# The planner's prices of transfers in a four-layer kernel: larger fixed part, lower rates

## Chip, core and metric

The kernel runs on one core of a Trainium2 chip. The metric is the device time of one execution in microseconds (us); the median of the runs is compared. TensorE is called PE, VectorE DVE, ScalarE ACT, GpSimd POOL and SyncE SP.

## What is computed

Four layers over `x`, 2 sequences of 1024 tokens with 128 features, all in float32. Each layer has the same frame:

```python
xn = _layernorm(x)
s = attention_like(xn)             # layer 0 Mamba scan, 1 linear attention, 2 SSD (chunked state space), 3 causal attention
g = _silu(feed_forward(xn))        # layers 0, 1, 2: experts, two of eight for each token; 3: a plain two-layer net
x = x + s * g
```

What matters for transfers lies in layers 0 and 2. In layer 0 the recurrence runs over 256 channels with 16 states each:

```python
dA = jnp.exp(dt_s[..., None] * A)
h = h * dA + (dt_s * x_s)[..., None] * B_s[:, None, :]
y = jnp.einsum('bds,bs->bd', h, C_s)
```

In layer 2 there are 32 heads of 64 channels, 128 states, and chunks, with a decay matrix inside a chunk and a state handed from chunk to chunk:

```python
M = Gm * Lmat
Y_diag = jnp.einsum('bclsh,bcshp->bclhp', M, h_c)
states = jnp.einsum('bhij,bjhpn->bihpn', dc, states)[:, :-1]
Y_off = jnp.einsum('bclhn,bchpn->bclhp', C_c, states) * sdo[..., None]
```

## The kernel before

**The work.** Tokens lie in 16 tiles of 128 (`X`). Layer 0 first normalises and routes, then scans four half sequences of 512 tokens (`inputs` and `step`, sixteen steps for each). A step needs 128 rows that are 32 channels times 4 states, so its operands are written to DRAM and read back replicated: `Dtd` (step width and its product with the input, stored at L1087, read into `dd` at L1230, for the very first ones straight from SBUF at L1228) and `BCd` (B and C, stored at L1056, read into `bc` at L1235). ACT makes `dA` (L1251), DVE `dBx` (L1243; every fourth on POOL, L1241) and the scan `hs` (L1252), POOL multiplies by C (L1256), PE folds the states (L1263). The experts of layer 0 (weights `fw`, L1133) run between the steps, and from the third half sequence on layer 1 of the first sequence too (weights `w13f` L775 and `w2e` L778).

Layer 2 works through 32 blocks of two heads (16 for each sequence) in pairs: `front` (projection, convolution; weights `wf` L1664, whose split halves are stored as `parts` at L1668 and read back by the second sequence at L1672), `weights` (decay rows `Srow` L1692 and `Mrow` L1693 are read from DRAM, PE makes `e_ps`, ACT its exponential, DVE `M`), `states` (`cd` L1712 is read replicated, DVE scans `st` at L1735) and `tail` (`so` L1751 is read replicated, then `yd_ps`, `yo_ps`, and every fourth block `wo_ps`). The next pair's `front` and `weights` are written before the present pair's `tail`. `Vd`, `Cd`, `So` and `Dd` are the DRAM tensors that these reads come from (L1537 to L1552). `gb` (L1810) reads the gate at the end of a sequence.

**Who sets the order.** Every transfer is issued on SP's queue. The order written in the program is only a start: `_issue_order` replaces it. It takes all instructions (`_operations`), with their dependences and a price for each (`_price` for engines; for a transfer also `op.wire`, its time on a wire that the plan shares out to one transfer at a time). `_forward` is a list scheduler: it plays the program by these prices, takes the ready instruction with the smallest key on every engine, opens a tile's buffer when its former user is done, and keeps a shared wire. `_backward` plays it from the end and gives each instruction its time to the end, which becomes the next round's key. Thirty such rounds are followed by 300 tries in which the keys within a stretch of 60 us are shaken at random; the order with the shortest planned time is kept, for all five queues, and the chip must follow it queue by queue.

A transfer's price has a fixed part, `_DMA`, and its bytes over a rate in bytes per ns. There are four kinds: one that doesn't replicate, one that replicates out of SBUF (`dd` from `dt`), one that replicates out of DRAM with more than two distinct rows (`bc` with 4, `dd` with 32), and one that does so with one or two (`so` with 1, `cd` with 2, broadcast parameter rows). A part of `_DMA` comes ahead of the wire and the rest behind it. `_backward` uses `_DMA + op.wire`. SP's own time for an issue is 500 ns, unchanged.

Of the kernel before, what the change touches and what calls it, by code (L numbers as in the profile page):

```python
# [72 lines left out]
_SAME = {"PE": -160.0, "DVE": 50.0, "Activation": 50.0, "Pool": 100.0, "SP": 0.0}  # L73
_TABLE = 1283.0
_SWITCH = 4000.0
_DMA = 1550.0
_SPELL = 3413.0
_LOW, _HIGH = 0.45, 0.8

# [11 lines left out]
def _table_of(ins):  # L91
    if ins.opcode != "Activation" or ins.func in (AF.Identity, AF.Copy, AF.Relu, AF.Abs, AF.Square):
        return None
    return "Exp" if ins.func in (AF.Exp, AF.Tanh) else str(ins.func)


def _elements(ap):
    n = 1
    for _, c in list(ap)[1:]:
        n *= c  # L100
    return n
# [51 lines left out]
def _operations(nc, slots):  # L153

    ops, users, past = [], {}, {}

    def in_psum(a):
        return a.tensor.name in slots and slots[a.tensor.name][3] == "PSUM"

    for ins in nc.cur_bb.bb.instructions:  # L160
        if type(ins).__name__.startswith("BassTile") or ins.opcode == "RegisterMove":
            continue
        op = _Op(len(ops), ins)
        reads, writes = ([a.bass_ap for a in x if getattr(a, "bass_ap", None) is not None] for x in (ins.ins, ins.outs))
        op.cost = _price(op, reads, writes, in_psum)
        op.table = _table_of(ins)
        op.columns, op.first, op.mate = set(), op, None
        if ins.opcode == "Matmult" and not ins.is_transpose and writes[0].ap[0][1] in (8, 32, 64):
            op.strip, op.area = writes[0].offset // (writes[0].ap[0][0] or 1), 1.0
            op.columns, op.strips = {(op.strip, writes[0].offset)}, {op.strip}  # L170
        op.wire = 0.0
        if op.dma:

            n, rows = 4, 1
            for _, c in writes[0].ap:
                n *= c
            again = any(s == 0 and c > 1 for s, c in reads[0].ap)
            for s, c in list(reads[0].ap)[:-1]:
                rows *= c if s else 1
            inside = reads[0].tensor.name in slots and slots[reads[0].tensor.name][3] != "DRAM"  # L180
            op.wire = n / (430.0 if not again else 200.0 if inside else 300.0 if rows > 2 else 170.0)
        for a, writing in [(a, False) for a in reads] + [(a, True) for a in writes]:
            name = a.tensor.name
            if name not in slots:
                continue
            space = slots[name][3]
            ap = [tuple(v) for v in a.ap]
            p0, p1, f0 = 0, 0, a.offset
            if space != "DRAM":
                row = _elements([(0, 0)] + [(0, d) for d in list(a.tensor.shape)[1:]])  # L190
                p0, f0 = divmod(a.offset, row)
                p1 = p0 + ap.pop(0)[1] - 1
            f1 = f0 + sum(abs(s) * (c - 1) for s, c in ap)
            if space == "PSUM":
                p0, p1, f0, f1 = 0, 127, 0, 4095
            log = past.setdefault(name, [])
            for q0, q1, g0, g1, other, wrote in log:
                if (writing or wrote or space == "PSUM") and other is not op and q0 <= p1 and p0 <= q1 and g0 <= f1 and f0 <= g1:
                    if other.engine != op.engine or other.dma:
                        lag = 0.0 if other.dma else _HOP[op.engine]  # L200
                    else:
                        lag = _SAME[op.engine] if wrote and not writing and op.engine != "PE" else -_AHEAD[op.engine]
                    op.after[other] = max(op.after.get(other, -1e3), lag)
            if writing:
                log[:] = [r for r in log if r[4] is op or not (p0 <= r[0] and r[1] <= p1 and f0 <= r[2] and r[3] <= f1)]
            log.append((p0, p1, f0, f1, op, writing))
            if name not in op.tiles:
                op.tiles.append(name)
                users.setdefault(name, []).append(op)
                if users[name][0] is not op:  # L210
                    op.after.setdefault(users[name][0], -1e3)

        mate = ops[-1] if ops else None
        if op.columns and mate is not None and mate.columns and mate.tiles[-1] == op.tiles[-1] and not mate.columns & op.columns:
            op.columns |= mate.columns
            if op.strip in mate.strips:
                op.cost += 10.0
            else:
                op.strips |= mate.strips
                op.cost = 25.0  # L220
            first = mate.first
            first.after.update({o: max(lag, first.after.get(o, -1e3)) for o, lag in op.after.items() if o.at < first.at})
            mate.mate, op.first = op, first
        ops.append(op)
    for op in ops:
        if op.columns and op.mate is None:
            op.cost += 87.0
    return ops, users
# [30 lines left out]
def _forward(ops, users, slots, behind, key):  # L259
# [22 lines left out]
    table, wire, port = None, 0.0, {"DVE": [0.0, 0.0], "Pool": [0.0, 0.0]}  # L282
    clock, spell, worked = 1.0, 0.0, 0.0

    def met(op, when):
        early[op] = max(early[op], when)
        need[op] -= 1
        if not need[op]:
            heapq.heappush(events, (early[op], 0, op.at, op))
# [17 lines left out]
    while events:  # L307
        now, kind, _, op = heapq.heappop(events)
        if kind == 2:
            for t in op.tiles:  # L310
                left[t] -= 1
                if not left[t]:
                    k = slots[t][:2]
                    free[k] += 1
                    freed[k].append(t)
                    open_tiles(k, now)
                    in_pool[k[0]] -= 1
                    if not in_pool[k[0]]:
                        for j, i in behind:
                            if j == k[0]:  # L320
                                waits[i] -= 1
                                for q in tags:
                                    if q[0] == i:
                                        open_tiles(q, now)
            continue
        e = op.engine
        if kind == 0:
            heapq.heappush(ready.setdefault(e, []), (key[op], op.at, op))
        if not ready.get(e) or idle.get(e, 0.0) > now:
            continue  # L330
        mate = orders[e][-1].mate if orders.get(e) else None
        held = [r for r in ready[e] if r[2] is mate] if mate is not None else []
        if held:
            op = mate
            ready[e].remove(held[0])
            heapq.heapify(ready[e])
        elif e == "PE" or e not in ("Activation", "DVE"):
            op = heapq.heappop(ready[e])[2]
        else:
            op = _next(ready[e], table, [max(0.0, t - now) for t in port["Pool"]] if e == "DVE" else (0.0, 0.0))  # L340
        cost = op.cost
        if op.table not in (None, table):
            table, cost = op.table, cost + _TABLE
        if op.lock:
            cost += max(0.0, *(port["Pool" if e == "DVE" else "DVE"][k] - now for k in op.lock))
            for k in op.lock:
                port[e][k] = now + cost
        if e == "PE":
            while now >= spell + _SPELL:
                clock = (1.0 if worked > _LOW * _SPELL else 0.5) if clock == 1.0 else (1.0 if worked > _HIGH * _SPELL else 0.5)  # L350
                spell, worked = spell + _SPELL, 0.0
            cost /= clock
            worked += cost * op.area
        start[op] = now
        orders.setdefault(e, []).append(op)
        idle[e] = now + (cost if e == "PE" or op.dma else max(cost - _AHEAD[e], 40.0))
        done = now + cost + (_AHEAD[e] if e == "PE" else 0.0)
        if op.dma:
            wire = max(wire, now + 0.4 * _DMA) + op.wire
            done = wire + 0.6 * _DMA  # L360
        end[op] = done
        for t in op.tiles:
            if t not in begun:
                begun.add(t)
                open_tiles(slots[t][:2], now)
        heapq.heappush(events, (idle[e], 1, op.at, op))
        heapq.heappush(events, (done + _HOP["PE"], 2, op.at, op))
        for other, lag in follow[op]:
            met(other, max(now, done + lag))
# [1678 lines left out]
```

## Time and profile before

| | |
|---|---|
| Median of 3 runs | 1190.09 us (1188.87 to 1194.23) |
| Profiled execution | 1188.86 us, its span 1187.1 us |
| Mean granted clock of PE | 0.939 |
| Instructions in the trace | 18167, of them 416 issues of transfers |
| Moved by DMA | 109.09 MB, 92 GB/s on average |
| HBM read, written | 91.52 MB, 14.29 MB |

The stages, as the trace shows them: 0 to 98 us loads, norms and routing; 98 to 450 the scan with the experts of layer 0 and the first sequence of layer 1; 450 to 560 layer 1's second sequence; 560 to 680 the passage into layer 2; 680 to 1100 its blocks; 1100 to 1187 layer 3.

How to read the lines that follow: Lnnn is a line of the kernel, a name such as `dd<-Dtd` is what is written and what is read, and SPq is SP's queue, which issues and waits but does no work. A row of waits names the one who waited, who ended the wait, the total in us, the number of times and the longest. The chain of waits is followed back from the last instruction, at each step to what released it.

| transfer | issues | KB each |
|---|---|---|
| `bc<-BCd` | 32 | 512 |
| `cd<-Dd` | 32 | 512 |
| `so<-So` | 64 | 256 |
| `dd<-Dtd` | 28 | 512 |
| `w13f`, `fw`, `w2e` | 16 each | 256, 192, 128 |
| `parts<-w_in_h`, `parts<-w_in_l` | 16 each | 128 |
| `Srow<-Cd`, `Mrow<-Vd` | 32 each | 16, 64 |

### The profile page before, as it was taken

How to read it: one execution, taken by the hardware profiler on the slowest of the kernel's cores; microseconds unless marked ns; L12 is line 12 of the kernel's file. 1: busy time of each engine (PE TensorE's matmuls, PEld its weight loads, DVE VectorE, ACT ScalarE, POOL GpSimd, SP SyncE). 2: the span in 40 equal slices, each digit the busy share in tenths (PEclk: the TensorE clock that was granted, in tenths of full speed). 3: DMA queues.
4: the chain of work that ended last, by engine and by line, in shares of the span. 5: the costliest groups of instructions: out<-in, count | busy, mean ns of one | idle time of the engine just before them, and what ended most of it. 6: DMA issues, size and time to landing. Idle time of an engine off the chain costs nothing.

```text
span 1187.1 us, 18167 instructions
## 1 busy us (share of the span) xinstructions
PE 1020.7 (86%) x6399; PEld 735.6 (62%) x6399; DVE 931.5 (78%) x1537; ACT 866.1 (73%) x1294; POOL 739.2 (62%) x776
## 2 busy tenths in 40 slices
PE   3997967979376889989779789999998999998998
PEld 2664523435033666778658576867676777776787
DVE  6734798997899896675776488888888999888666
ACT  4556785785877894574847689888898988877654
POOL 6564598895987375232151158797995978899311
PEclk9998997999567989999959899999999999999999
DMA  3003445352552113020030333445354444442000
GB/s 109 8 21 101 125 120 182 123 186 99 189 177 83 51 62 100 1 82 23 5 106 32 87 100 96 111 119 149 101 141 95 125 107 112 107 111 73 19 9 28
DMA packets 58846, 109.09 MB, mean 92 GB/s; under 512 B 6274, under 2 KB 31746, under 8 KB 58628
## 3 DMA queue, kind: packets, MB, share of 16 engines
q1 hardware_dynamic: 58756, 107.93, 31.6%
q8 instruction: 51, 0.84, 0.3%
q14 instruction: 39, 0.32, 0.1%
HBM read 91.52 MB, written 14.29 MB: 89 GB/s over the span
## 4 chain that ended last, share of the span: by engine, by line
PE 34%; DVE 10%; ACT 9%; issue 4%; DMA 3%; POOL 2%; SPq 0%; POOLq 0%; DVEq 0%; ACTq 0%
PE wo_ps L1781 4%; PE yd_ps L1757 3%; PE u_ps L1734 3%; PE yo_ps L1762 3%; DVE h L1419 2%; PE e_ps L1698 2%; PE y_ps L799 2%; DVE st L1735 2%; PE ht_ps L1719 1%; DMA so<-So 1%; PE y_ps L1895 1%; PE y_ps L1646 1%; PE av_ps L1925 1%; ACT e_ps L1699 1%; DVE M L1701 1%
## 5 line engine op out<-in xcount | busy, mean ns | idle before, releaser
L1256 POOL TENSOR_TENSOR hs<-hs,bc 128x512 f32<-128x512 f32 x128 | 161.0, 1278 | 48.6 <-DVE hs L1252 28.8
L1419 DVE SCALAR_TENSOR_TENSOR h<-in_ps,w,h 128x1023 f32<-128x1023 f32 (+2 forms) x96 | 121.1, 1271 | 5.7 <-ACT h L1416 5.5
L1251 ACT ACTIVATE dA<-dd,negA 128x512 f32<-128x512 f32 x128 | 87.4, 688 | 31.8 <-DVE hs L1252 25.4
L1735 DVE TENSOR_TENSOR_SCAN st<-cd,u_ps 128x512 f32<-128x512 f32 x64 | 77.8, 1215 | 19.4 <-PE u_ps L1734 8.7
L1701 DVE SCALAR_TENSOR_TENSOR M<-e_ps,GT 128x1024 f32<-128x1024 f32 x64 | 77.0, 1214 | 10.5 <-ACT e_ps L1699 10.3
L1768 POOL TENSOR_TENSOR h<-h,so 128x384 f32<-128x384 f32 (+1 forms) x64 | 73.0, 1144 | 19.1 <-DVE so L1767 18.6
L1769 POOL TENSOR_TENSOR h<-h,sg 128x512 f32<-128x512 f32 x64 | 82.9, 1300 | 0.8
L1252 DVE TENSOR_TENSOR_SCAN hs<-dA,last,dBx 128x512 f32<-128x512 f32 x64 | 79.9, 1271 | 2.9 <-ACT dA L1251 2.0
L799 PEld LDWEIGHTS y_ps<-w2e,hh 128*128 128x128 f32 x512 | 72.4, 199 | 14.7 <-DVE hh L791 3.8
L799 PE MATMUL y_ps<-w2e,hh 128*128 128x128 f32 x512 | 78.1, 288 | 1.9 <-DVE acc L804 0.9
L1723 POOL TENSOR_TENSOR hdd<-htok,dtd 128x512 f32<-128x512 f32 x64 | 67.1, 1051 | 20.3 <-ACT htok L1722 15.4
L1774 POOL TENSOR_TENSOR ssq<-ssq,so 128x512 f32<-128x512 f32 x60 | 76.6, 1286 | 3.0 <-ACT so L1773 2.9
L1757 PE MATMUL yd_ps<-M,htok 128*64 128x128 f32 x1024 | 70.7, 280 | 8.0 <-DVE M L1701 5.6
L1252 DVE TENSOR_TENSOR_SCAN hs<-dA,dBx 128x512 f32<-128x512 f32 x64 | 75.7, 1211 | 2.1 <-ACT dA L1251 1.1
L1734 PEld LDWEIGHTS u_ps<-hdd,Btok 128*128 128x128 f32 x448 | 63.3, 193 | 16.8 <-issue 6.0
L1762 PE MATMUL yo_ps<-Cf,stc 128*128 128x128 f32 x448 | 70.7, 280 | 2.1 <-DVE h L1765 0.9
L1734 PE MATMUL u_ps<-hdd,Btok 128*128 128x128 f32 x448 | 69.8, 281 | 2.8 <-POOL stc L1737 1.3
L1762 PEld LDWEIGHTS yo_ps<-Cf,stc 128*128 128x128 f32 x448 | 62.3, 191 | 13.4 <-issue 4.7
L1757 PEld LDWEIGHTS yd_ps<-M,htok 128*64 128x64 f32 x1024 | 55.1, 137 | 24.4 <-issue 7.0
L1243 DVE TENSOR_TENSOR dBx<-dd,B_ps 128x1024 f32<-128x1024 f32 x48 | 57.9, 1209 | 12.2 <-PE xz_ps L623 4.7
L1699 ACT ACTIVATE e_ps<-e_ps 128x1024 f32<-128x1024 f32 x64 | 64.3, 1011 | 1.9 <-PE e_ps L1698 1.4
L1263 PE MATMUL y_ps<-hs,fold 128*32 128x512 f32 x256 | 52.9, 758 | 14.1 <-DVE ln_t L591 9.2
(535 smaller groups left out, 3190.7 us busy)
## 6 DMA issues: line engine op xcount, KB each, us to landing
bc<-BCd SPq DMA_DIRECT2D x32, 512.0 KB
cd<-Dd SPq DMA_DIRECT2D x32, 512.0 KB
so<-So SPq DMA_DIRECT2D x64, 256.0 KB
dd<-Dtd SPq DMA_DIRECT2D x28, 512.0 KB
w13f<-in_w13d_dram SPq DMA_DIRECT2D x16, 256.0 KB
Dtd<-dt SPq DMA_DIRECT2D x7, 512.0 KB
fw<-in_fwd_dram SPq DMA_DIRECT2D x16, 192.0 KB
dd<-dt SPq DMA_DIRECT2D x4, 512.0 KB
```

Of the source, the lines that this page charges most:

```text
L799: nc.tensor.matmul(y_ps[:, j * P : (j + 1) * P], hh[:, c, j * P : (j + 1) * P], w2e[:, c * P : (c + 1) * P], start=(c == 0), stop=(c == 1))
L1251: nc.scalar.activation(dA, dd[:, r, 0, :], AF.Exp, scale=negA[:, n, r : r + 1])
L1252: nc.vector.tensor_tensor_scan(hs[:, r, :], dA, dBx[:, r, :], last[:, n, r : r + 1] if h else 0.0, ALU.mult, ALU.add)
L1256: nc.gpsimd.tensor_tensor(hs[:, r, :], hs[:, r, :], cs[:, 0, :], ALU.mult)
L1419: nc.vector.scalar_tensor_tensor(dst[:, n:], ps[:, : S - n], w[:, k : k + 1], dst[:, n:], ALU.mult, ALU.add)
L1701: nc.vector.scalar_tensor_tensor(M, ps, 3.0e38, G, ALU.min, ALU.mult)
L1734: nc.tensor.matmul(pv[:, j, :], Btok[:, c, :], hdd[:, c, :], start=True, stop=True)
L1735: nc.vector.tensor_tensor_scan(st.rearrange("p f j -> p (f j)"), cd[:, half].rearrange("p h w -> p (h w)"), ps, 0.0, ALU.mult, ALU.add)
L1757: nc.tensor.matmul(yd[64 * k : 64 * (k + 1), j * P : (j + 1) * P], htok[:, 4 * q + j, 64 * k : 64 * (k + 1)], Ms[q][:, k, j * P : (j + 1) ...
L1762: nc.tensor.matmul(yo[:, j * P : (j + 1) * P], stc[:, c - 1, :], Cf[:, c * P : (c + 1) * P], start=True, stop=True)
L1769: nc.gpsimd.tensor_tensor(y, y, sg[:, cols], ALU.mult)
L1774: nc.gpsimd.tensor_tensor(ssq[:, cols], ssq[:, cols], so[:, cols], ALU.add)
```

## The change

The fixed part of a transfer's price goes from 1550 to 2150 ns. The rates go from 430 to 300 (not replicated), from 200 to 190 (replicated out of SBUF) and from 300 to 230 (replicated out of DRAM, over two rows); 170 for one or two rows stays. Of the fixed part, 0.6 instead of 0.4 now lies ahead of the wire: 1290 ns instead of 620 ahead of it and 860 instead of 930 behind it. Nothing else in the program is touched; the prices act through the order that `_issue_order` writes.

```diff
-_DMA = 1550.0
+_DMA = 2150.0
...
-            op.wire = n / (430.0 if not again else 200.0 if inside else 300.0 if rows > 2 else 170.0)
+            op.wire = n / (300.0 if not again else 190.0 if inside else 230.0 if rows > 2 else 170.0)
...
         if op.dma:
-            wire = max(wire, now + 0.4 * _DMA) + op.wire
-            done = wire + 0.6 * _DMA
+            wire = max(wire, now + 0.6 * _DMA) + op.wire
+            done = wire + 0.4 * _DMA
```

## Prediction

> **What bounds the kernel now.** The page first, for the whole span: the engines' busy time and the share of the 16 DMA engines that the program's one transfer queue takes.
>
> ```profile
> PE 1020.7 (86%) x6399; PEld 735.6 (62%) x6399; DVE 931.5 (78%) x1537; ACT 866.1 (73%) x1294; POOL 739.2 (62%) x776
> q1 hardware_dynamic: 58756, 107.93, 31.6%
> ```
>
> No engine is full and the wires are a third used, so an average says little. The second view cuts the span into stages (columns: length, busy time of PE, weight loads, DVE, ACT, POOL, granted clock, DMA share, GB/s).
>
> ```profile
> 98.00:450.00 352.00, 268.98 (x1314) 147.59 (x1313) 295.86 (x380) 269.28 (x438) 264.13 (x229) 0.85 0.39 126
> 560.00:680.00 120.00, 97.44 (x593) 78.65 (x592) 78.41 (x176) 79.17 (x119) 27.10 (x36) 0.85 0.20 58
> 680.00:1100.00 420.00, 398.01 (x2898) 304.01 (x2897) 366.31 (x418) 359.16 (x467) 341.41 (x332) 1.00 0.42 109
> ```
>
> In layer 2 (680 to 1100) PE is busy 398 of 420 us at full clock: at most 22 us can be won from waits there. In the scan of layer 0 (98 to 450) DVE leads with 296 of 352 us. In the passage into layer 2 (560 to 680) nobody is full and the clock is 0.85. The third view is the waits, those that a landing transfer ended, summed (us, times, longest):
>
> ```profile
> ACT w_in_h L609 <- DMA so<-So: 7.3, 1, 7.3
> POOL u L1007 <- DMA BCd<-bc_rows: 6.1, 1, 6.1
> ACT dA L1251 <- DMA dd<-dt: 6.0, 1, 6.0
> DVE dBx L1243 <- DMA dd<-Dtd: 4.3, 3, 2.6
> ```
>
> PE has no such row. Going through the engines' idle times of 0.7 us and over one by one, 22 were ended by a landing, 61 us over all engines. Fourth, the chain that ended last; its transfers of 3 us or more (start, length) are these six, 33 us together, which is the page's "DMA 3%":
>
> ```profile
> 462.71 4.30 DMA w<-in_w_dram
> ...
> 661.05 3.18 DMA so<-So
> ...
> 723.38 4.75 DMA so<-So
> ...
> 827.72 4.92 DMA cd<-Dd
> ...
> 902.34 8.88 DMA gb<-g2d
> ...
> 1037.54 7.07 DMA so<-So
> ```
>
> The chain begins only at 436 us (its shares add to 62%). Around these links PE was mostly busy with other work: 9.8 of 10 us at 457 to 467, 9.5 of 10 at 1036 to 1046, 6.4 of 8 at 826 to 834. They are links of waiting, not 33 us to be won.
>
> **The change, part by part.** No instruction is added or removed; every one keeps its operands. Only the prices by which the planner orders the five queues change, so all that can move is order: who stands before whom on PE, DVE, ACT, POOL and SP.
>
> Prices. A transfer of n bytes cost 1550 ns plus n over its rate; now 2150 ns plus n over a lower one. Times in us from issue, old to new: `bc` and `dd` from DRAM (512 KB, 300 to 230) 3.30 to 4.43; weights `w13f` (256 KB, 430 to 300) 2.16 to 3.02; `gb` (512 KB) 2.77 to 3.90; `dd` from SBUF (200 to 190) 4.17 to 4.91; `parts` (128 KB) 1.85 to 2.59; `Srow` (16 KB) 1.59 to 2.20. `cd` and `so`, 96 transfers and the longest in layer 2, keep 170, since their source has one or two rows: 4.63 to 5.23 and 3.09 to 3.69. Not all kinds slow down.
>
> What the trace says of these prices: I took from its semaphore records, per transfer, the time from the start of the issue to the last landing. Medians: `bc` 4.06 (3.88 where nothing else was in flight), `dd` from DRAM 5.29, `so` 6.32 (shortest 3.43), `cd` 5.87 (shortest 4.65), `w13f` 2.94, `dd` from SBUF 9.0, `gb` 3.74 and 8.9, `parts` of the high halves 1.93, `Srow` 1.59. With the planner's formula put on the recorded issue times, its one shared wire included, the old prices end before the real landing in 89% of the transfers (median 0.7 us too early), the new ones in 35% (median 0.3 us too late). The old ones fit stores and tiny loads on an idle wire; the new ones fit loads under company. So consumers that the old plan puts too early will mostly stand later, and loads are asked for earlier.
>
> The Trainium skill speaks against the rates: "DMA: Bandwidth & Descriptors", section "Anatomy of one DMA — SWDGE (gpsimd) path", fits 2.0 us plus bytes over 436 GB/s (for GpSimd's path), an estimate of 3.2 us for `bc`. By it the fixed part should rise and the rates stay, and the sum below would keep only its fixed parts; the 3.88 us measured here for `bc` is above it.
>
> Against the new prices there is the wire: over the scan the old rates price its transfers at about 135 us (`bc` 56, `dd` 59, `Dtd` 8.5, weights some 11), and the DMA share of 0.39 times 352 is 137. The new rates make it about 176. Over the whole span it is 411 old, 484 new and 375 recorded (31.6% of 1187.1). The new plan spaces loads wider than the wire needs; the cost of that is in the rivals.
>
> The sum. An idle time that a landing ended shrinks at most by what its transfer's price rose, and counts where nothing covers it. In the scan: ACT's `dA` 5.96 at 118.1 (rise 0.74), DVE's `dBx` 1.52 and 2.60 and POOL's 1.57 and 2.95 at 158 to 197 (rise 1.13 each): 0.74 + 4 x 1.13 = 5.3 us. I count it in full, since DVE, ACT and POOL feed one another step by step there. In layer 2 and its entry: `w_in_h` 7.32 behind `so` (0.60), `so` 0.85 behind `cd` (0.60), `gb` 2.67 (1.13), `h` 1.77 behind `w_in_h` (0.74), `so` 0.70 and 1.47 (0.60 each): 4.3 us. PE runs through most of them, so I count half, 2.1. The other eleven idle times (first loads, `BCd` 6.06 at 98.0, weights of later layers) have rises that add to about 10 us; I count none: the loads stand at the front of SP's queue already or PE has work. Sum: -7.4 us, bounds 0 (all of it covered) and -19 (all 22 count). What is late next there is DVE in the scan and PE in layer 2, so no more than this follows.
>
> At nothing I cost: the overpriced `parts`, `Srow` and `Mrow`. They are hidden by the look-ahead, in which block pair k+2's weights are made under pair k's tails; without that cover it would be 0.6 us for each of 16 pairs, 9.6 us. Also at nothing, the moves of SP's issues themselves (0.3 to 0.5 us each): SP stands idle for most of the span.
>
> The profiled execution took 1188.86, 1.76 over its span of 1187.1, and lies 1.2 below the median of 1190.09. 1188.86 - 7.4 = 1181.5, on the median's footing 1182.7: 1183, the case's own range 1171 (-19) to 1192 (+2).
>
> **Rivals.** The slower one: a queue blocked at its head. SP issues in order, and its own waits are long already:
>
> ```profile
> SPq L1133 <- PE p L1154: 111.6, 11, 42.0
> ...
> SPq L1235 <- POOL hs L1256: 101.3, 25, 10.5
> ```
>
> A dearer load is asked for earlier; where its buffer is still read, it stands at the head of SP's queue, and every transfer behind it waits, first `BCd`, `Dtd`, `dd` and `bc` at the three changes of half sequence in the scan. The planner knows when a buffer comes free only by its own prices; the rival decides when a buffer is freed later than planned by more than the roughly 1 us by which the load was moved up. Its price is read from the two waits already seen at such a place, 6.06 (`BCd`) and 5.96 (`dd` from SBUF): two of three boundaries give 12 us, 1202. One alone gives 1196. All three give 18 us, and if PE falls to half clock meanwhile for three of the 3.41 us windows in which the trace shows its clock to change (at most 1.7 us of its work lost in each), 1213. For it: POOL and DVE in the scan have no slack to catch up. Against it: most of these waits, 42 us among them, delay nobody now.
>
> The second: the waits only change their name. Where PE or DVE leads, a transfer that lands in time lets the next instruction wait for PE or DVE. The -7.4 shrinks to within 2 us: 1190 (1188 to 1192). For it speaks PE's 95% in layer 2; against it the scan, where DVE sits idle 56 us. That the plan stays as it was is not possible in full, since every transfer's price enters every key; that it changes little in layer 2, because `so` and `cd` keep their rate, belongs to this case.
>
> **How the numbers follow.** About 0.5%, 6 us, is what a measurement of this kernel can tell from no change: faster means below 1184, slower above 1196. Forecast 0.58 (below 1184 0.36, near 0.20, slower 0.02, its centre lying close to the line); the waits renamed 0.10, all near; the blocked queue 0.32, all slower. That makes 0.36, 0.30 and 0.34. The forecast's range of 1171 to 1192 holds about half of all chance; up to 1210 it takes in most of the blocked queue, and no more than 2 in 10 is left out.
>
> **What would show it.** Right: idle time ended by landings falls from 61 to about 45 us, `dA`'s wait for `dd` and `dBx`'s waits shrink by about 1 us each, the scan ends some 5 us earlier, PE's time in layer 2 stays at 398 us. Blocked queue: SP rows for L1133, L1230 or L1235 with single waits of over 10 us just ahead of a scan step, and ACT or DVE idle behind `dd` or `bc` for more than 6 us. Renamed: the landing waits fall and the stages keep their lengths. Wrong altogether: the landing waits stay and a stage without transfers moves by more than 6 us, the last one (1100 to 1187, DMA share 0.06) above all; then order among compute instructions, which these rows can't price, made the time.

## The result, and the profile after

The changed kernel takes 1201.59 us (median; 1190.32 to 1209.67), the kernel before 1188.47 (1182.81 to 1198.96) in the same comparison: a ratio of 1.0092, 95% interval 1.0066 to 1.0118. The ratio leaves out the three slowest executions of the changed kernel; the two medians alone would give 1.011. Slower by 0.9%: outside the forecast's own 1171 to 1192 us, within the 1210 us that the prediction allowed for its rivals, and on the side that had 0.34. The profiled execution of the changed kernel took 1195.42 us, its span 1193.7: 6.6 us over the span before, and itself 6 us below its kernel's median.

The page of the changed kernel, busy times, the transfer queue and the chain by engine:

```profile
PE 1022.3 (86%) x6399; PEld 739.0 (62%) x6399; DVE 937.7 (79%) x1537; ACT 869.8 (73%) x1296; POOL 738.5 (62%) x776
q1 hardware_dynamic: 58756, 107.93, 30.6%
PE 42%; ACT 17%; DVE 15%; issue 6%; POOL 3%; DMA 1%; SPq 0%; POOLq 0%; DVEq 0%; ACTq 0%
```

The work is the same to within 6.2 us for each engine; the packets took no longer (30.6% against 31.6%). Transfers fell from 3% of the chain to 1%. The waits that a landing ended (us, times, longest), answering to those shown before:

```profile
ACT dA L1251 <- DMA dd<-dt: 9.8, 2, 5.5
ACT w_in_h L609 <- DMA so<-So: 7.1, 1, 7.1
ACT fw_h L609 <- DMA fw<-in_fwd_dram: 5.7, 4, 3.0
DVE dBx L1243 <- DMA dd<-dt: 5.0, 1, 5.0
```

`BCd` (6.1) and `dd<-Dtd` (4.3) are gone from the list; what is left stands at the scan's entrance, behind `dd` from SBUF, which took 9.0 us in the trace before and which the new price of 4.91 us still undershoots. There the waits grew: `dA`'s from 6.0 to 9.8 us, and `dBx` has one of 5.0 that was not in the list before. Over all engines the idle times of 0.7 us and over that a landing ended went from 61.0 us (22 of them) to 47.9 (15). Now the stages, cut where each trace has them: scan (first to last `hs`), layer 2 (first `e_ps` to last `wo_ps`), layer 3. First the kernel before, then the changed one (length, busy time of PE, weight loads, DVE, ACT, POOL, granted clock, DMA share, GB/s):

```profile
126.70:447.80 321.10, 246.94 (x1229) 133.76 (x1232) 285.55 (x361) 252.78 (x413) 250.87 (x204) 0.85 0.37 124
...
671.90:1100.80 428.90, 404.82 (x2929) 308.65 (x2930) 371.29 (x422) 367.20 (x475) 344.26 (x335) 0.99 0.42 107
1100.80:1187.10 86.30, 78.26 (x549) 69.07 (x547) 57.61 (x167) 48.13 (x77) 14.91 (x24) 0.99 0.07 19
```

```profile
125.10:443.90 318.80, 247.05 (x1247) 137.19 (x1247) 285.93 (x370) 254.99 (x415) 251.83 (x204) 0.87 0.37 127
...
670.60:1103.00 432.40, 404.09 (x2924) 307.14 (x2924) 373.46 (x422) 372.53 (x479) 343.93 (x333) 1.00 0.40 106
1103.00:1193.70 90.70, 81.50 (x553) 71.05 (x552) 57.34 (x167) 48.88 (x77) 15.83 (x26) 0.98 0.06 18
```

Up to the first `e_ps` the changed kernel is 1.3 us ahead (670.6 against 671.9). Then it loses 3.5 us in layer 2 and 4.4 in layer 3. In layer 2 PE is busy as long and stands idle longer (432.4 - 404.1 = 28.3 us against 24.1). In layer 3 most of the loss is busy time: nearly the same number of matmuls took 81.5 us instead of 78.3, at a granted clock of 0.98 instead of 0.99, and the idle time went from 8.0 to 9.2 us. Layers 2 and 3 together: 515.2 us before, 523.1 after. Layer 3 moves little by DMA (share 0.06). This is the direction that the prediction named as "wrong altogether", though not its signs as written: the landing waits did fall, and layer 3 moved by 4.4 us, not by more than 6.

### The profile page after: what moved, and what is told of

The parts are those of the page before. It is cut to its first block, busy times and chain, and to the rows that moved or that the text cites. A ratio compares the mean times of both kernels' runs of the same rounds, so it can differ in the third digit from the quotient of the medians.

```text
span 1193.7 us, 18169 instructions
## 1 busy us (share of the span) xinstructions
PE 1022.3 (86%) x6399; PEld 739.0 (62%) x6399; DVE 937.7 (79%) x1537; ACT 869.8 (73%) x1296; POOL 738.5 (62%) x776
## 3 DMA queue, kind: packets, MB, share of 16 engines
q1 hardware_dynamic: 58756, 107.93, 30.6%
## 4 chain that ended last, share of the span: by engine, by line
PE 42%; ACT 17%; DVE 15%; issue 6%; POOL 3%; DMA 1%; SPq 0%; POOLq 0%; DVEq 0%; ACTq 0%
PE wo_ps L1781 4%; PE u_ps L1734 3%; PE yd_ps L1757 3%; PE y_ps L799 3%; DVE hs L1252 3%; DVE h L1419 2%; PE yo_ps L1762 2%; ACT L790 2%; ACT dA L1251 2%; PE e_ps L1698 2%; PE ht_ps L1719 2%; ACT L1251 2%; DVE st L1735 1%; PE y_ps L1895 1%; PE in_ps L621 1%
## 5 line engine op out<-in xcount | busy, mean ns | idle before, releaser
L1251 ACT ACTIVATE dA<-dd,negA 128x512 f32<-128x512 f32 x128 | 87.3, 687 | 37.5 <-DVE hs L1252 26.8
L790 ACT ACTIVATE hh<-pg 128x512 f32<-128x512 f32 x64 | 37.6, 597 | 47.5 <-PE pg L623 42.9
L1734 PEld LDWEIGHTS u_ps<-hdd,Btok 128*128 128x128 f32 x448 | 60.5, 191 | 15.9 <-issue 4.4
L1762 PEld LDWEIGHTS yo_ps<-Cf,stc 128*128 128x128 f32 x448 | 60.4, 191 | 11.7 <-issue 4.1
L1781 PE MATMUL wo_ps<-h,w 128*128 128x512 f32 x128 | 63.0, 598 | 2.6 <-DVE so L1767 2.2
```

What stands on the lines that cost most here:

```text
L1251: nc.scalar.activation(dA, dd[:, r, 0, :], AF.Exp, scale=negA[:, n, r : r + 1])
L1734: nc.tensor.matmul(pv[:, j, :], Btok[:, c, :], hdd[:, c, :], start=True, stop=True)
L1762: nc.tensor.matmul(yo[:, j * P : (j + 1) * P], stc[:, c - 1, :], Cf[:, c * P : (c + 1) * P], start=True, stop=True)
L1781: nc.tensor.matmul(ps, Wo[:, j, :], y[:, cols], start=(n == 0), stop=(n == 3))
```

## The experiments

Every time is set against runs of the kernel before on the same chip, and that kernel's median was between 1186.27 and 1188.90 us in these comparisons, so ratios compare better than medians. The expectations set three theories against each other: A, the level of the prices costs the time; B, any new order is a fresh draw; C, the blocked queue of the prediction. "Layers 2 and 3" is the stretch from the first `e_ps` to the end in the profiled execution.

**Another seed.** The 300 random tries that follow the thirty rounds get another seed; prices stay.

```diff
-    rng = random.Random(1)
+    rng = random.Random(2)
```

> The kernel before, its old prices untouched, with the seed of the 300 random tries 2 instead of 1. Theory A (the new prices themselves cost about 11 us): a new seed under the old prices changes little, so 1183 to 1194 us. Theory B (any new draw of the order moves the time by about 1%, and the kernel before holds a lucky draw): 1195 to 1210 us, and the stages that differ need not be those with transfers. Theory C (the rival on record, a blocked transfer queue): as A.

> The changed kernel with seed 2. Theory A: 1195 to 1210 us, slower by 6 to 17 us than the old prices with the same seed. Theory B: anywhere from 1180 to 1210 us, its difference to the old prices with seed 2 of either sign. Theory C: 1195 to 1210 us, with waits of the transfer queue of over 10 us just ahead of idle scan steps in its trace.

> The kernel before with seed 3. Theory A: 1183 to 1194 us. Theory B: 1180 to 1210 us, most likely above 1194. Theory C: as A.

> The changed kernel with seed 3. Theory A: 1195 to 1210 us. Theory B: 1180 to 1210 us, and over the three seeds the mean difference of new to old prices is below 6 us, smaller than the spread over the seeds of one price. Theory C: 1195 to 1210 us with the same queue waits.

| | median us | ratio, interval | layers 2 and 3, us |
|---|---|---|---|
| old prices, seed 2 | 1186.97 | 0.9986 (0.9957 to 1.0016) | 515.3 |
| old prices, seed 3 | 1182.64 | 0.9966 (0.9938 to 0.9994) | 515.1 |
| new prices, seed 2 | 1198.89 | 1.0082 (1.0052 to 1.0111) | 524.1 |
| new prices, seed 3 | 1191.69 | 1.0026 (0.9997 to 1.0055) | 523.2 |

New prices are slower with every seed, by 9 to 13 us (seed 1 is that of the two kernels themselves), and layers 2 and 3 take 515 us under the old and 523 to 524 under the new ones. Taken alone that looks like theory A, and theory B's 1195 us or more for old prices with seed 2 did not come. But a seed only shakes the keys within stretches of 60 us around an order that the thirty rounds have set, and those rounds know no seed: three seeds are three finishes of one base order.

**The same level, another base.** The fixed part moves by 10 or 20 ns, far less than the landings of one kind of transfer differ among themselves (`bc`: 3.4 to 7.0 us in the trace before), but it feeds the thirty rounds.

```diff
-_DMA = 1550.0
+_DMA = 1560.0
```

(and 1540, 1570; for the changed kernel 2130, 2140, 2160)

> The kernel before with a fixed part of 1560 ns instead of 1550, all else as before. A change of 10 ns says nothing about the chip, but it feeds the thirty rounds that set the base of the order, which another seed does not touch. Theory A (the size of the prices decides): 1182 to 1192 us, and the second sequence of layer 2 keeps the 216 us that it has under the old prices with all three seeds. Theory B (every new base order is a fresh draw of about 1%): as likely above 1194 as below, and that stage leaves 216 us by 4 or more.

> The changed kernel with a fixed part of 2140 ns instead of 2150. Theory A: 1192 to 1206 us, the second sequence of layer 2 at 223 to 226 us as under the new prices with all three seeds. Theory B: anywhere from 1178 to 1210 us.

> The kernel before with a fixed part of 1540 ns instead of 1550: one more fresh base order at the old level of prices. Theory B (the order of layers 2 and 3 in the kernel before is a lucky draw, 515 us from the first e_ps to the end under all three seeds): that stretch takes 519 to 525 us here too, as it did with 1560 (522.7), and the time is 1186 to 1198 us. Theory A (the level of the prices decides): 515 to 517 us, 1180 to 1190 us, and 1560 was the exception.

> The changed kernel with 2160 ns instead of 2150. Theory A: 1195 to 1205 us. Theory B: a fresh draw of the base, 1185 to 1205 us; layers 2 and 3 at 519 to 525 us.

> One more base order at the old level (1570 ns). Old-level draws so far lie at ratios 1.000 (1550), 1.0015 (1560) and 1.0028 (1540), new-level draws at 1.0092, 1.0062 and 1.0061. Theory A: ratio 0.997 to 1.004. Theory B: 0.997 to 1.010, the two groups begin to overlap.

> One more base order at the new level (2130 ns). Theory A: ratio 1.005 to 1.011. Theory B: 0.997 to 1.010.

| fixed part, ns | median us | ratio, interval | scan | layers 2 and 3 |
|---|---|---|---|---|
| 1540 | 1192.95 | 1.0028 (1.0003 to 1.0053) | 318.4 | 521.4 |
| 1550 (before) | 1188.47 | 1 | 321.1 | 515.2 |
| 1560 | 1190.73 | 1.0015 (0.9984 to 1.0047) | 318.8 | 522.7 |
| 1570 | 1196.64 | 1.0058 (1.0032 to 1.0084) | 323.3 | 516.3 |
| 2130 | 1184.90 | 0.9969 (0.9942 to 0.9997) | 323.3 | 515.5 |
| 2140 | 1196.46 | 1.0062 (1.0030 to 1.0093) | 332.0 | 523.5 |
| 2150 (changed) | 1201.59 | 1.0092 (1.0066 to 1.0118) | 318.8 | 523.1 |
| 2160 | 1194.34 | 1.0061 (1.0036 to 1.0087) | 334.2 | 515.0 |

Old prices with 10 ns more or less lose the 515 us, and with 20 ns more nearly have them again (516.3); new prices with 10 ns more or 20 less have them. Layer 2 and layer 3 of these two (1560 first, then 2160):

```profile
667.80:1105.40 437.60, 409.96 (x2929) 312.92 (x2929) 378.54 (x424) 369.44 (x478) 341.10 (x333) 0.99 0.40 105
1105.40:1190.50 85.10, 79.20 (x550) 68.73 (x548) 57.29 (x167) 48.00 (x76) 18.33 (x27) 0.99 0.06 20
```

```profile
677.90:1106.70 428.80, 404.74 (x2925) 309.58 (x2926) 373.58 (x422) 365.15 (x473) 341.41 (x332) 1.00 0.41 107
1106.70:1193.00 86.30, 79.21 (x553) 69.14 (x551) 57.43 (x167) 48.58 (x77) 18.33 (x27) 1.00 0.06 19
```

So the level of the prices does not decide those 8 us; which base order the planner starts from does. Theory A's sign for 2140 ns, 223 to 226 us for the second sequence of layer 2 (from the 65th of its 128 `e_ps`), did not come either: it took 215.2 us there, and the 8 us lay in the first. Those 8 us are not the whole time: 1570 and 2160 ns keep 515 or 516 us and are slower than the kernel before by 0.6%, because they reach the first `e_ps` at 681.2 and 677.9 us instead of 671.9. Within the old level the ratios spread over 0.58% (1.0058 - 1), within the new one over 1.23%, and the best of all eight, 1184.90 us, has the new prices. The means of the four are 1.0025 and 1.0046, 0.2% apart, which four draws of such a spread can't tell from nothing. One thing the table leaves open: two of the new scans (332.0 and 334.2 us) are longer than any old one, so the new prices may lengthen the scan; up to the first `e_ps` the four old ones take 667.8 to 681.2 us and the four new ones 668.2 to 677.9.

**One part of the change alone.**

```diff
 # fixed_only: the fixed part, old rates and old split
-_DMA = 1550.0
+_DMA = 2150.0
 # rates_only: the rates, old fixed part and old split
-            op.wire = n / (430.0 if not again else 200.0 if inside else 300.0 if rows > 2 else 170.0)
+            op.wire = n / (300.0 if not again else 190.0 if inside else 230.0 if rows > 2 else 170.0)
```

> Only the fixed part raised, 1550 to 2150 ns; old rates and old split. In layer 2 the heavy transfers so and cd take their whole rise from this part. Theory A with the fixed part as cause: 1195 to 1206 us, layer 2's second sequence at 222 us or more. Theory A with the rates as cause: 1182 to 1193 us. Theory B: neither is bound to hold, and the parts do not add up.

> Only the rates lowered (430, 200, 300 to 300, 190, 230); fixed part and split as before. Theory A with the rates as cause (wires planned fuller than they are): 1195 to 1206 us. Theory A with the fixed part as cause: 1182 to 1193 us. Theory B: as for the fixed part alone.

Fixed part 1194.77 us, ratio 1.0071 (1.0033 to 1.0109), layers 2 and 3 522.1; rates 1191.13, 1.0029 (0.9997 to 1.0060), 519.4. The times come close to "theory A with the fixed part as cause" (1194.77 lies 0.2 us below its range, 1191.13 inside), but the second sequence of layer 2 took 217.1 us with the fixed part alone and not 222 or more. Beside the table above both are two more draws, and nothing is settled by them alone. The new split of the fixed part was not tried alone.

**Two plans spliced.** Both plans are made; every queue follows one of them up to the planned start of the first matmul of layer 2's first tail, and the other with what is left.

```diff
+CUTS = [(1, "tail_0_0"), (0, None)]        # new plan, then old; the other way round for its counterpart
...
+    for which, name in cuts:
+        until = plans[which][1][next(op.at for op in ops if op.ins.name in name and op.engine == "PE")] if name else 1e18
+        part = {k for k, t in enumerate(plans[which][1]) if t < until} - done
+        done |= part
+        for e, o in plans[which][2].items():
+            orders[e] += [k for k in o if k in part]
```

> No price at work after the cut but another order: both plans are made as the two kernels make them; up to the planned start of layer 2's first tail every queue follows the changed kernel's plan, from there on what is left follows the plan of the kernel before. Both theories place the loss behind the cut, so layers 2 and 3 should go back to 514 to 518 us (changed kernel 523.1) and the time to 1184 to 1192 us. If the loss came from the first half, by what it leaves behind, it stays at 1195 us or more.

> The counterpart: the plan of the kernel before up to the same cut, the changed kernel's plan for the rest. Loss behind the cut: layers 2 and 3 take 521 to 526 us and the time is 1194 to 1204 us. Loss ahead of the cut: 1184 to 1192 us.

Layer 2 and layer 3, new plan then old (1194.05 us, ratio 1.0051, 1.0025 to 1.0078), and after it old plan then new (1199.9 us, 1.0104, 1.0049 to 1.0158):

```profile
676.50:1104.70 428.20, 403.34 (x2929) 307.10 (x2930) 371.28 (x422) 364.73 (x473) 344.77 (x335) 1.00 0.42 107
1104.70:1191.10 86.40, 78.19 (x548) 69.01 (x547) 57.59 (x167) 48.17 (x77) 14.89 (x24) 0.99 0.07 19
```

```profile
668.70:1104.80 436.10, 406.94 (x2924) 309.76 (x2924) 373.76 (x422) 375.58 (x481) 344.27 (x334) 0.99 0.41 105
1104.80:1196.30 91.50, 82.89 (x552) 72.52 (x552) 57.66 (x167) 48.87 (x77) 15.79 (x26) 0.96 0.06 18
```

428.2 + 86.4 = 514.6 us with the old plan behind the cut, 436.1 + 91.5 = 527.6 with the new one; the unspliced kernels have 515.2 and 523.1. The loss in layers 2 and 3 lies in the order of the instructions there. But the first splice came out at 1194.05, above the 1192 expected and below the 1195 of the other case: the first half under the new plan costs something too. Its trace reaches the first `e_ps` at 676.5 us, where the profiled execution of the changed kernel, with the same order so far, took 670.6.

**The changed kernel once more.** No edit; a second trace of the same order.

> The changed kernel itself, for a second trace of the same order. Its recorded execution (1195.42 us) lies 6 us under its median (1201.59), so some stage was short by luck. If that was the scan (318.8 us there, 325.4 in the splice that follows the same order as far as that), a second trace shows the scan at 322 to 328 us with more time at half clock than the 85 us of the first, and layers 2 and 3 again at 522 to 525 us. If the 6 us lie in layers 2 and 3, those take 526 us or more and the scan about 319.

1204.08 us, ratio 1.0140 (1.0105 to 1.0174). Its scan, layer 2 and layer 3:

```profile
122.00:446.60 324.60, 256.47 (x1246) 141.09 (x1247) 286.27 (x369) 255.04 (x416) 251.78 (x204) 0.84 0.37 125
669.40:1101.70 432.30, 405.51 (x2924) 308.66 (x2924) 373.40 (x422) 372.56 (x479) 343.94 (x333) 0.99 0.41 106
1101.70:1195.40 93.70, 84.26 (x553) 74.11 (x552) 57.41 (x167) 48.83 (x77) 15.80 (x26) 0.95 0.06 18
```

The scan came out as expected: 324.6 us, with 105.8 us at half clock where the first trace had 85.3 (counted from the trace's clock records). Layer 3 took 93.7 us at a clock of 0.95, which makes 526.0 us for both layers, one us more than the expectation allowed with such a scan. This execution was recorded at 1197.08 us, again 7 us below its kernel's median, so where the slower executions lose those last us stays open. The same program came out at 1.0092 in one comparison and at 1.0140 in another: ratios half a percent apart can be one kernel measured twice.

**The level taken further.** Two more steps up, and one step down.

```diff
 # dearer
-_DMA = 2150.0
+_DMA = 3350.0
-            op.wire = n / (300.0 if not again else 190.0 if inside else 230.0 if rows > 2 else 170.0)
+            op.wire = n / (180.0 if not again else 170.0 if inside else 150.0 if rows > 2 else 170.0)
 # cheaper
-_DMA = 1550.0
+_DMA = 950.0
-            op.wire = n / (430.0 if not again else 200.0 if inside else 300.0 if rows > 2 else 170.0)
+            op.wire = n / (760.0 if not again else 210.0 if inside else 430.0 if rows > 2 else 170.0)
```

> The changed kernel's prices raised by about two more steps of the same size: fixed part 3350 ns; rates 180, 170 (out of SBUF), 150, and 170 as ever. If the level of the prices itself costs time (theory A), this costs more: 1205 to 1225 us, most of it in the scan, where the wire is then priced fuller than the stage is long. If only the draw of the order counts (theory B): 1185 to 1202 us like all the others, and the landing waits are close to zero.

> The kernel before with prices lowered by one step: fixed part 950 ns; rates 760, 210, 430, 170. Theory A as a straight line through old and new: 1175 to 1186 us. Theory A with an optimum near the old prices: 1195 us or more, with landing waits over the 61 us of the kernel before. Theory B: 1185 to 1202 us.

Dearer: 1212.0 us, 1.0166 (1.0105 to 1.0226). Cheaper: 1225.57 us, 1.0280 (1.0219 to 1.0342). The landing waits do what the prices say; the lines are those of the dearer plan, all that its list of waits has, and then the longest of the cheaper one:

```profile
ACT gw_h L609 <- DMA f<-in_f_dram: 3.9, 1, 3.9
ACT qW L951 <- DMA w<-in_w_dram: 2.5, 1, 2.5
```

```profile
ACT fw_h L609 <- DMA fw<-in_fwd_dram: 19.9, 11, 4.7
ACT dA L1251 <- DMA dd<-dt: 10.0, 2, 7.6
DVE so L1767 <- DMA so<-So: 7.3, 4, 4.2
```

Idle times of 0.7 us and over that a landing ended: 10.1 us dearer, 79.5 cheaper. Yet both are slower, as theory A had it and theory B (1185 to 1202 us) had not. The cheaper plan reaches the first scan step at 138.8 us instead of 126.7 and takes 337.0 us for the scan; the dearer one takes 336.5 us for the scan with no landing wait of 0.3 us or over in it. Far off, then, the level seems to matter on either side, with one order tried on each: the cheaper one lies clear of every order at the two levels, the dearer one's interval takes in the changed kernel's second measurement. Between the level before and the level after no difference in the whole time is shown.

## Why the prediction was wrong

**Forecast faster; it is slower.** The step on transfers came out by its number: landing waits were to fall from 61 to about 45 us and fell to 47.9, and inside the scan, idle times of 0.3 us and over included, from 12.3 us to 0.5, more than the 5.3 of the sum. Its first term went the other way: `dA`'s wait of 5.96 us behind `dd` from SBUF, ahead of the first `hs`, was to shrink by 0.74 and became 9.8. And that the new prices made the total fall is not shown. Counted the same way, the other orders at the old level have 44.3 and 47.1 us (seeds 2 and 3), 64.1, 31.2 and 43.8 (1540, 1560 and 1570 ns); those at the new level have 39.4 and 43.7 (seeds 2 and 3), 60.6, 42.9 and 49.5 (2130, 2140 and 2160 ns). The two groups overlap, and the fastest order at the new level, 2130 ns, waits as long as the kernel before. Only the far levels stand apart, with 79.5 and 10.1 us. So the agreement at 47.9 is in good part luck.

The reading of the prices against the recorded landings holds in the main, since the old ones mostly end too early; two of its medians come out lower from the same records, `so` at 4.74 us instead of 6.32 and `cd` at 5.52 instead of 5.87, still above their new prices of 3.69 and 5.23. The Trainium skill ("DMA: Bandwidth & Descriptors", section "Anatomy of one DMA — SWDGE (gpsimd) path") fits 2.0 us plus bytes over 436 GB/s, for GpSimd's path. The prediction took from it that the fixed part should rise and the rates stay. The run nearest to that is the one with the fixed part alone; at 1.0071 it is one draw among the others, and no run here ranks the two parts.

**The step that failed first is the -5.3 us counted "in full" in the scan.** The scan took 321.1 us before, and 318.8 and 324.6 in the two traces after (325.4 in the splice that begins with the same order). The waits changed their name, as the second rival had it, and in the very stage that the prediction cited against it. DVE leads there, and its 4.3 us behind `dd<-Dtd` are gone; its scan `hs` waits longer for ACT's `dA` instead. The rows of the scan, before:

```profile
DVE hs L1252 <- ACT dA L1251: 3.1, 8, 0.6
ACT dA L1251 <- DVE hs L1252: 25.4, 25, 4.4
```

and after:

```profile
DVE hs L1252 <- ACT dA L1251: 9.3, 11, 1.4
ACT dA L1251 <- DVE hs L1252: 26.8, 22, 4.4
```

DVE worked 286 us in either trace and stood idle 35.6 us before (321.10 - 285.55) and 32.9 after (318.80 - 285.93); in the second trace after, its wait for `dA` is 9.4 us and its idle time 38.3. "What is late next is DVE" was said, and should have been priced: here the landing waits of an engine that also waits for other engines were not won.

**The step that was missing is the larger one: the price of a new order.** The sum put nothing for instructions changing places, although the diff can do nothing else. What it cost here is 7.9 us in layers 2 and 3 (523.1 - 515.2), shown by the splices to come from the order there and by 1560 and 2160 ns to be a matter of the draw. The medians are 13.1 us apart; where the rest of that lies stays open, as said above. How much a new order costs could not be read from one trace, as the prediction said; that there is such a price, of either sign, could, and it deserved a case of its own with a chance, not a last sentence. The eight base orders lie between 0.997 and 1.009 of the kernel before, six of the seven others above it (1560 ns not clearly: its interval takes in 1).

One place shows how such a loss looks. The chain of waits at the end of layer 2 in the changed kernel (start, length):

```profile
1098.18 1.22 POOL h L1768
1099.40 2.44 POOL h L1769 x2
1101.85 0.71 POOL ssq L1774
1102.56 0.45 issue
1103.01 1.29 POOL ssq L1774
1104.31 0.69 POOL qk_w_l L610
1105.00 0.04 issue
1105.04 0.79 PE qk_ps L621
```

`qk_w_l`, the low half of layer 3's weights, needs nothing of layer 2. The old plan had it on POOL at 1089.0, in the shadow of layer 2, and PE's first product of layer 3 at 1092.7, ahead of the last `wo_ps`; the new plan puts both behind layer 2's tail, at 1104.2 and 1105.0; under all three seeds PE's first product of layer 3 comes after the last `wo_ps`. How much of layer 3's 4.4 us this one slip makes was not tried. It can't be all: with seeds 2 and 3 layer 3 took 87.7 and 87.3 us. The long layer 3 of the changed kernel's own order comes with a lower clock in all three of its traces, 90.7 us at 0.98, 93.7 at 0.95 and 91.5 at 0.96 in the splice, against 0.99 or 1.00 with the other seeds and other fixed parts; what makes the clock fall there was not tried either.

**The rival that came true by its number did not by its mechanism.** The blocked queue was priced at 1202, and the median is 1201.59; but the waits of the queue that it named did not grow. After the change:

```profile
SPq L1235 <- POOL hs L1256: 101.3, 25, 8.2
SPq L1133 <- PE p L1154: 91.4, 12, 46.1
```

L1133 waited 111.6 us before and 91.4 after, L1235 101.3 in both; other lines rose or fell (L1056, the store of `BCd`, from 11.7 to 29.2 us), and the sum over the queue went from 981 to 992. No scan step idles more than 5.5 us behind `dd`, and none behind `bc`. Without the mechanism the agreement is an accident.

## What to carry to other kernels

When a change can act only through a planner's order, price the new draw first: vary a constant by an amount that cannot matter (here 10 ns) and see how far the time moves; a difference smaller than that says nothing about the constant. Another seed of a local search is not another draw when a deterministic part ahead of it sets the base. Waits for transfers that vanished here, in a stage with three busy engines, came back under other names; ask for the stage's length, not for its waits. And before a fall in waits is put down to the change, see how far they move between draws: here from 31 to 64 us at one level of prices. The experiments left two orders slightly faster than both kernels: old prices with seed 3 (1182.64 us, 0.9966, 0.9938 to 0.9994) and new prices with 2130 ns (1184.90, 0.9969, 0.9942 to 0.9997), one at either level of prices.

## What the runs showed of the hardware

One order of instructions gave scans of 318.8 and 324.6 us in two executions, with 85.3 and 105.8 us at half clock; PE's busy time there grew from 247.1 to 256.5 us with the same 1246 or 1247 matmuls. In the list of the changed kernel's 20 executions the four below 1196 us have a mean granted clock of 0.942 to 0.947 and the eight above 1205 us one of 0.932 to 0.935; but three between 1196 and 1198 us have 0.933 to 0.937, so the clock does not tell the time alone. Nor does it in the scan: the splice that begins with the same order took 325.4 us there with 92.0 us at half clock and PE busy for 247.3 us, and DVE busy for 290.6 instead of 285.9. Why one order takes scans 6 us apart stays open.
